# A graph layer with its edges in sorted order: one quad of hot nodes moved to the end of the list

## The chip, the core and the metric

The kernel runs on one core of one Trainium2 chip. The metric is the device time of one execution in microseconds (us). The engines have short names: PE is TensorE (matmul), PEld its weight loads, DVE is VectorE, ACT is ScalarE, POOL is GpSimd and SP is SyncE, which issues most transfers. Each engine takes its own instructions in order and waits for others through semaphores.

## The reference

There are 12,500 nodes of 128 features and 400,000 edges, sorted by destination. A destination is 12500 times the square of a uniform number, so nodes with low numbers are hot: they have many edges. Each edge has a length. Only edges shorter than 10 have any effect, which are 71,145 of these inputs.

```python
rbf = jnp.exp(-(distances[:, None] - centers) ** 2 / (2.0 * width * width))
cut = 0.5 * (jnp.cos(jnp.pi * distances / CUTOFF) + 1.0) * (distances <= CUTOFF)
W = (jax.nn.silu(rbf @ fw1 + fb1) @ fw2 + fb2) * cut[:, None]
messages = (h[src] @ pw + pb) * W
agg = jax.ops.segment_sum(messages, dst, num_segments=num_atoms)
y = h + (jax.nn.silu(agg @ mw1 + mb1) @ mw2 + mb2)
out = _layernorm(x + y)          # h is x
```

## The kernel before

**Packing.** Seven chunks of edges (bounds QB = 0, 13, 24, 46, 69, 91, 114, 141 in quads) are compacted on DVE: the edges shorter than 10 are put in order, and written are their source rows (`srci`), places among nodes (`dl`, `f_dl`), lengths (`near_d`), cut factors (`cut`) and the base node of each half quad (`base_i`). Chunks 1 to 6 are packed beside the main loop.

**The main loop** has NL = 139 steps, one for each quad of 4 x 128 edges. POOL gathers the rows of proj = x@pw + pb, one indirect DMA for 128 edges (L1048), four to a quad; for eight quads, named in `SINGLY`, one of the four is fetched row by row through SP instead (L1038). ACT makes the radial functions for two quads at a time (L1094, L1095), PE multiplies by fw1 (L1103), ACT applies silu (L1109), PE multiplies by fw2 with the bias (L1117, L1120), and DVE multiplies by the gathered rows, which gives the message (L1131; for the last quad in four pieces). DVE also builds a one-hot matrix of destinations times the cut factor (`hot`, L1143, in `place`). PE multiplies message by one-hot into PSUM (`sums`, L1163, in `sum_up`), and DVE adds the result to aggT, which holds all nodes' sums, at a base read into a register (L1196, in `add`). The two halves of a quad have a base each. `added(q)` says up to which quad the additions have come at step q, and `keep_busy` puts filler matmuls into PE's queue (L1350).

**Node blocks.** Since the edges are sorted, a tile of 128 nodes is final once the quads that reach it are added. From step 70 on, blocks of nodes run beside the edges: `node_first` (PE L1204 and L1205, then silu on ACT L1209), `node_second` (PE L331, L334), `node_stats` (DVE L1225, which forms 2x + y, and the statistics L1230), `deviations` (L1237 to L1241, the last on ACT), `scales` (L1248, L1249, whose result is `by`), and `normalize` (DVE or POOL L1260, or ACT L1263, and the store L173). Blocks are four tiles; the last ones, in `TAIL`, have 4, 4, 2, 3, 2 and 3 tiles and start at tiles 80, 84, 88, 90, 93 and 95; they are called by these numbers. Tile 97, the last one, has 84 nodes. `READY` gives how many steps ahead of the end a block's first product is put into the queue.

**The end.** After the loop stand the last quad's addition, blocks 90, 93 and 95, and a branch (`tc.If(some > 0)`, L1640) round a general path, which these inputs don't take. Ahead of it stands a hint on the branch for each of five engines.

The order on each engine is that in which the Python code calls these functions; a clock kept by the planner places the packing work and the gathers between them.

Of the kernel before, what the change touches and what calls it, by code (L numbers as in the profile page):

```python
# [20 lines left out]
P = 128  # L21
# [22 lines left out]
NL = 139  # L44
AHEAD = 3
# [25 lines left out]
SINGLY = (22, 45, 62, 67, 86, 102, 118, 133)  # L71
# [7 lines left out]
READY = {80: 9, 84: 6, 88: 5, 90: 3, 93: 2}  # L79
# [4 lines left out]
def kernel(  # L84
# [57 lines left out]
    x_sb, loaded = {}, [0]  # L142

# [6 lines left out]
    def rows(t0, n=None):  # L150
        n = n or TAIL.get(t0, 4)
        return [min(P, N - t * P) for t in range(t0, min(t0 + n, NT))]
# [15 lines left out]
    def node_dma(t0, sb, dr, store, n=None, eng=nc.sync):  # L168

        for a, m, k in alike(rows(t0, n)):  # L170
            d = dr[(t0 + a) * P:(t0 + a) * P + m * k].rearrange("(p t) f -> p t f", p=k)
            s = sb[:k, a:a + m]
            eng.dma_start(d, s) if store else eng.dma_start(s, d)  # L173

# [636 lines left out]
    def unpack(c):  # L811
# [69 lines left out]
        def later(more=0.0):  # L881

            if c or known[0] >= DIRECT // QT:
                awake[c] = clock[0] + (5.0 if known[0] >= QB[c + 1] else 1.0 if c == 0 else 2.5) + more
# [31 lines left out]
        known[0] = QB[c + 1]  # L916
        yield 0
        mine = [q for q in SINGLY if QB[c] <= q < QB[c + 1]]
        if mine:
            at_row = work.tile([64, P], I32, name="at_row", bufs=2)  # L920
            nc.vector.tensor_scalar(at_row[:np_], f_src[:, :P], float(4 * H), None, op0=OP.mult)
            for q in mine:
                p = 2 * (q - QB[c])
# [16 lines left out]
        nc.vector.tensor_scalar(f_dl, part, base, None, op0=OP.subtract)  # L940
        yield from to_places(f_dl, dl)
# [22 lines left out]
        nc.vector.scalar_tensor_tensor(inside, f_dl, float(WIDTHS[c]), inside, op0=OP.is_lt, op1=OP.mult,  # L964
# [77 lines left out]
    def fetch(q, idx=None, table=None, js=range(QT)):  # L1042
        got = quad_sb[place_of(q) if q >= 0 else 0]
        for j in js:
            if q in SINGLY and j == 0:
                continue
            i = srci[:, 2 * q + j // 2, j % 2:j % 2 + 1] if idx is None else idx[:, j:j + 1]
# [24 lines left out]
    def radials(to):  # L1072

        while next_o[0] < min(to, -(-NL // 2)):
# [3 lines left out]
            a, b = 4 * o, 2 * quads(o)[-1] + 2  # L1078
# [3 lines left out]
    def chunk_of(q):  # L1082
        return max(c for c in range(NC_) if QB[c] <= q)
# [54 lines left out]
    def place(q):  # L1138

        hot = own(q, "hot", 1)  # L1140
        for j in reversed(range(QT)):
            at = 2 * q + j // 2, slice(j % 2, j % 2 + 1)
# [26 lines left out]
    def base_of(q, ks=(0, 1)):  # L1169
        for k in ks:  # L1170
            if k == windows(q):
                break
            _, v = nc.values_load_multi_w_load_instructions(  # L1173
                base_i[0:1, 2 * q + k:2 * q + k + 1], engines=[mybir.EngineType.DVE],
# [4 lines left out]
    def bases_of(q0, q1):  # L1179

        _, v = nc.values_load_multi_w_load_instructions(
            base_i[0:1, 2 * q0:2 * q1], engines=[mybir.EngineType.DVE],
# [91 lines left out]
    def finish(every):  # L1274

        for t0 in every:
# [6 lines left out]
            normalize(*ready.pop(0))  # L1283
# [3 lines left out]
    blocks = [*range(0, min(TAIL), 4), *TAIL]  # L1287
# [8 lines left out]
    def nodes(q):  # L1296
# [5 lines left out]
        for k, t0 in enumerate(early):  # L1302
            if begin[t0][0] - 5 == q:
                load_x(t0)
            if begin[t0][2] == q:
                if k % 4 == 0:
                    st_of[0] = statistics()
                node_stats(t0, st_of[0][:, k % 4 * 4:])
# [14 lines left out]
        if q == NL - 3:  # L1323
            node_stats(88, st_of[3][:, 8:])
            dev_of.append(deviations([84, 88], st_of[3][:, 4:]))
            nc.scalar.activation(warm, half_pi, AF.Silu)
        if q == NL - 2:
            node_second(90)
            for k in (1, 2):
                st_of[k] = statistics()  # L1330
            scales(*dev_of.pop(0))
            for _ in (84, 88):
                normalize(*ready.pop(0))

    st_of, deep, dev_of = {}, [], []

    def tail(q):

        for t0, k in READY.items():
            if q == NL - k:  # L1340
                assert done_to(2 * added(q + 1)) >= (t0 + TAIL[t0]) * P
# [49 lines left out]
    def pack_until(us, among=2):  # L1391

        while clock[0] < us and todo and todo[0] < among:
            have = [c for c in todo[:3] if c < among and (c == 0 or c - 1 in sent or c == todo[0])]
            have.sort(key=lambda c: 0 if c in sent and known[0] < QB[c + 1] else 1)
# [69 lines left out]
    while known[0] < QB[2]:  # L1465
# [21 lines left out]
    for q in range(NL - 1):  # L1487
# [3 lines left out]
        if q == NL - 2:  # L1491
            bases_of(q, NL)
# [21 lines left out]
        if q > NL - 5:  # L1514
            keep_busy(2)
        sum_up(q, msg)
        now = range(added(q), added(q + 1))
        for k in now if q < NL - 2 else ():
            base_of(k, (0,))
        if q < NL - 2:  # L1520
            place(q + 1)
        if q == NL - 4:
            place(NL - 1)
        if q == NL - 2:
            for j in range(QT):
                sum_up(NL - 1, message(NL - 1, (j, j + 1)), (j,))
        for k in now:
            if q < NL - 2:
                base_of(k, (1,))
# [11 lines left out]
        if todo:  # L1541
            pack_until(max(there_at[q + 1], clock[0] + (PACK_US if known[0] >= QB[3] else EARLY_US)), NC_)
# [7 lines left out]
    add(NL - 1)  # L1550
    node_first(95)
    node_stats(90, st_of[1])
    node_second(93)
    tc.mark_branch_hint_location("rest", some, [
# [123 lines left out]
```

## Time and profile before

| | us |
|---|---|
| median of 3 runs | 723.49 |
| lowest and highest | 722.11 and 725.21 |
| the profiled execution | 723.36 |
| its span in the trace | 721.6 |
| busy time of POOL in the span | 534.3 (74%) |
| busy time of PE, DVE, ACT | 588.0, 560.8, 399.6 |

The mean granted clock of PE was 0.912. A row of the timeline has the start, the time it took, the engine, the line, the operation, output and inputs, the shape, how many such instructions the row stands for, and in brackets how long the engine had been idle before it and what ended that. A row of the windows has the stretch, its length, the busy time (and number) of PE, PE's weight loads, DVE, ACT and POOL, the granted clock of PE (1.00 is full rate), the busy share of the DMA engines and GB/s.

### The profile page before, as it was taken

The numbers are of one execution on the slowest core, as the hardware profiler recorded it, in microseconds if no ns is written. First come the engines' busy times: TensorE is split into PE (matmuls) and PEld (weight loads), VectorE is DVE, ScalarE is ACT, GpSimd is POOL, SyncE is SP. The second block draws the span as 40 slices with busy tenths as digits, with TensorE's granted clock in tenths as the row PEclk, the third lists the DMA queues.
The fourth block names the chain that finished last, engine by engine and source line by source line (L and its number), as shares of the span: only waits on it lengthen the run. The fifth ranks groups of instructions, "written<-read, shape, count | busy, mean of one in ns | idle before, by whom it ended". The sixth has DMA issues, their size and how long they took to land.

```text
span 721.6 us, 13649 instructions
## 1 busy us (share of the span) xinstructions
PE 588.0 (81%) x3519; PEld 462.7 (64%) x3519; DVE 560.8 (78%) x1737; ACT 399.6 (55%) x569; POOL 534.3 (74%) x572
## 2 busy tenths in 40 slices
PE   6777787898888878788498898999977878888974
PEld 6766455776766657667376676777755656556753
DVE  8898879787988999899589996868555545655684
ACT  6547624474545576465338355859744744574483
POOL 7777777777777777777777777777777777777771
PEclk9999786998988999999769998999997989999997
DMA  8996433334333433342333343544433433255242
GB/s 273 331 303 196 143 115 86 79 110 125 97 101 87 127 98 105 99 126 86 98 102 112 101 117 101 148 124 141 128 97 112 142 99 99 82 170 138 63 141 66
DMA packets 53103, 91.37 MB, mean 127 GB/s; under 512 B 13824, under 2 KB 20576, under 8 KB 53018
## 3 DMA queue, kind: packets, MB, share of 16 engines
q1 hardware_dynamic: 34466, 53.20, 22.1%
q0 software_dynamic: 17840, 36.77, 20.2%
q8 instruction: 29, 0.48, 0.3%
q10 hardware_dynamic: 712, 0.46, 0.2%
q14 instruction: 56, 0.46, 0.2%
HBM read 74.59 MB, written 15.79 MB: 125 GB/s over the span
## 4 chain that ended last, share of the span: by engine, by line
DVE 30%; PE 24%; DMA 14%; issue 13%; POOL 11%; ACT 4%; DVEq 2%; SPq 0%; ACTq 0%; POOLq 0%
POOL quad L1048 11%; DMA quad<-proj,srci 9%; PE ph L1103 7%; DVE hot L1143 5%; PE bank L1120 5%; PE sums L1163 5%; DVE msg L1131 3%; PE bank L334 3%; DVE aggT L1196 2%; DVE r_d L509 2%; DVE bank L515 2%; DVEq L1173 2%; PE bank L1117 2%; DVE nodes L519 2%; DVE quad L1143 1%
## 5 line engine op out<-in xcount | busy, mean ns | idle before, releaser
L1048 POOL DMA_INDIRECT quad<-proj,srci x421 | 400.0, 950 | 128.4 <-issue 105.5
L1120 PEld LDWEIGHTS bank<-fw_sb,s 128*128 128x128 f32 x1112 | 159.3, 207 | 69.3 <-issue 62.1
L1109 ACT ACTIVATE s<-ph 128x1024 f32<-128x1024 f32 x70 | 71.3, 1018 | 176.5 <-PE ph L1103 176.4
L1120 PE MATMUL bank<-fw_sb,s 128*128 128x128 f32 x1112 | 159.7, 290 | 0.0
L1103 PE MATMUL ph<-rbf,w_sb 102*128 102x512 f32 x278 | 146.7, 653 | 7.7 <-ACT rbf L1095 3.8
L1163 PEld LDWEIGHTS sums<-hot,msg 128*128 128x128 f32 x816 | 109.5, 200 | 57.7 <-issue 27.6
L1143 DVE TENSOR_SCALAR hot<-iota_n,dl,cut 128x80 f32<-128x80 f32 (+4 forms) x408 | 108.3, 339 | 24.7 <-PE sums L1163 22.2
L1163 PE MATMUL sums<-hot,msg 128*128 128x80 f32 (+4 forms) x816 | 111.3, 281 | 17.7 <-DVE msg L1129 10.0
L1117 PE MATMUL bank<-fb_b,ones_b 96*128 96x512 bf16 x139 | 56.0, 403 | 50.9 <-DVE msg L1131 31.0
L1048 POOL DMA_INDIRECT x<-proj,srci x79 | 74.8, 947 | 24.1 <-issue 20.1
L1131 DVE TENSOR_TENSOR msg<-bank,quad 128x512 f32<-128x512 f32 (+1 forms) x82 | 55.5, 676 | 40.3 <-DMA quad<-proj,srci 36.0
L1103 PEld LDWEIGHTS ph<-rbf,w_sb 102*128 102x128 f32 x278 | 52.5, 210 | 48.1 <-issue 38.7
L1196 DVE TENSOR_TENSOR aggT<-aggT,sums 128x80 f32 (+4 forms) x209 | 53.7, 257 | 30.9 <-PE bank L1205 11.7
L1094 ACT ACTIVATE rbf<-d,rbf_bias,rbf_scale 102x512 f32<-102x512 f32 x70 | 56.2, 803 | 20.1 <-DMA d<-near_d 20.1
L1048 POOL DMA_INDIRECT quad<-in_x_dram,srci x48 | 48.1, 1003 | 15.5 <-issue 12.5
L334 PEld LDWEIGHTS bank<-pw_sb,xT 128*128 128x128 f32 (+1 forms) x292 | 42.1, 208 | 8.0 <-issue 4.2
L1095 ACT ACT_TABLE_LOAD x35 | 44.9, 1283 | 0.6
L1109 ACT ACT_TABLE_LOAD x35 | 44.9, 1283 | 0.6
L1131 DVE TENSOR_TENSOR quad<-bank,quad 128x512 f32<-128x512 f32 (+2 forms) x40 | 25.3, 632 | 25.6 <-DMA quad<-proj,srci 21.6
L1095 ACT ACTIVATE rbf<-rbf 102x512 f32<-102x512 f32 x70 | 44.1, 630 | 1.5
L334 PE MATMUL bank<-pw_sb,xT 128*128 128x128 f32 (+1 forms) x292 | 42.6, 293 | 0.6 <-ACT xT L984 0.6
L1143 DVE TENSOR_SCALAR quad<-iota_n,dl,cut 128x128 f32<-128x128 f32 (+3 forms) x148 | 40.6, 352 | 3.0 <-issue 1.8
(273 smaller groups left out, 803.8 us busy)
## 6 DMA issues: line engine op xcount, KB each, us to landing
d<-near_d SPq DMA_DIRECT2D x70, 256.0 KB
dl<-proj SPq DMA_DIRECT2D x1024, 0.5 KB
x<-in_x_dram SPq DMA_DIRECT2D x46, 256.0 KB
quad<-proj,srci POOLq DMA_INDIRECT x421
proj<-hp SPq DMA_DIRECT2D x24, 256.0 KB
out_dram<-x SPq DMA_DIRECT2D x22, 256.0 KB
r_d<-in_edge_weight_dram SPq DMA_DIRECT2D x5, 256.0 KB
r_dst<-in_dst_dram SPq DMA_DIRECT2D x5, 256.0 KB
```

What stands on the lines that cost most here:

```text
L334: nc.tensor.matmul(to[:m, k, :], lT[:, k * P:k * P + m], w, start=False, stop=(k == a + c - 1))
L1048: ins = nc.gpsimd.indirect_dma_start(out=got[:, j, :], out_offset=None, in_=proj if table is None else table, in_offset=bass.IndirectOffse ...
L1094: nc.scalar.activation(rbf[:u], d[:u], AF.Square, bias=rbf_bias[:u], scale=rbf_scale[:u])
L1095: nc.scalar.activation(rbf[:u], rbf[:u], AF.Exp, scale=-1.0 / (2.0 * width * width))
L1103: nc.tensor.matmul(ph[:, h, :], w1_sb[:2 * KR, h, :], rbf[:2 * KR], start=True, stop=True)
L1109: nc.scalar.activation(s[:, :n], ph[:, :n], AF.Silu)
L1117: nc.tensor.matmul(pu, ones_b[:, :P], bias_b["fb2"].rearrange("k j f -> k (j f)"), start=True, stop=False)
L1120: nc.tensor.matmul(pu[:, j * H:(j + 1) * H], s[:, j * P:(j + 1) * P], fw2_sb, start=False, stop=(j == QT - 1))
L1131: nc.vector.tensor_mul(msg[:, a:b, :], pu_of[q].rearrange("p (j f) -> p j f", j=QT)[:, a:b, :], got_of[q][:, a:b, :])
L1143: nc.vector.tensor_scalar(hot[:, j, :wide(q)], iota_n[:, :wide(q)], dl[:, at[0], at[1]], cut[:, at[0], at[1]], op0=OP.is_equal, op1=OP.mult)
L1163: ins = nc.tensor.matmul(pa[:, k * W:k * W + wide(q)], msg[:, j, :], hot[:, j, :wide(q)], start=(j % n == 0), stop=(j % n == n - 1))
L1196: nc.vector.tensor_add(to, to, pa[:, k * W:k * W + wide(q)])
```

## The change

Quad 26, whose edges go to nodes 437 to 472, all in tile 3, leaves its place and becomes the last step, 138 (`LAST`, `quad_of`, `steps`); every quad behind it is handled one step earlier. Tile 3 is therefore not part of block 0 any more but a block of its own (`END`, one tile), loaded near the end and done last. Chunk 2's check of places gets narrower bounds for quad 26, in four small DVE operations (`that`, `lim`, `upto`). Since block 95 no longer waits for the last quad, blocks 90, 93 and 95 go ahead, between the messages of the last two quads: block 90's statistics ahead of step 137's one-hot (`late_nodes`), 93 and 95 between the four pieces of the last message (`last_step`). Blocks 93, 95 and END have one common group of deviations. Block 88 and block 90 are normalised on POOL, and so is 93. The fillers of the steps NL-3 and NL-2 are gone. The last quad's sums have one window, 80 nodes wide, where they had two of 128. The hint on the branch is given for DVE, PE and POOL only, and the general path ends in one `finish(blocks)` where it had three.

```diff
-SINGLY = (22, 45, 62, 67, 86, 102, 118, 133)
+SINGLY = (22, 44, 62, 67, 86, 102, 118, 133)
-READY = {80: 9, 84: 6, 88: 5, 90: 3, 93: 2}
+READY = {80: 9, 84: 6, 88: 5, 90: 4, 93: 3}
+LAST = 26
+END = 3
+SIZES = {0: 3, END: 1, **TAIL}
...
+    def quad_of(q):
+        return q if q < LAST or q >= NL else LAST if q == NL - 1 else q + 1
...
+    def late_nodes():
+        node_stats(90, st_of[3][:, 10:])
+        deep.append(deviations([84, 88, 90], st_of[3][:, 4:]))
+        nc.scalar.activation(warm, half_pi, AF.Silu)
+        st_of[1] = statistics()
+    def last_step(q, msg):
+        bases_of(q, NL - 1)
+        tc.mark_branch_hint_location("rest", some, [
+            mybir.EngineType.DVE, mybir.EngineType.PE, mybir.EngineType.Pool])
+        sum_up(q, msg)
+        scales(*deep.pop(0))
+        node_second(93)
+        def last(j):
+            sum_up(NL - 1, message(NL - 1, (j, j + 1)), (j,))
+        normalize(*ready.pop(0))
+        last(0)
+        add(q)
+        last(1)
+        node_first(95)
+        node_stats(93, st_of[1])
+        last(2)
+        node_second(95)
+        for n in (2, 3):
+            normalize(*ready.pop(0), on=range(n), v=nc.gpsimd)
+        last(3)
+        add(NL - 1)
+        node_first(END)
+        node_stats(95, st_of[1][:, 2:])
+        node_second(END)
+        node_stats(END, st_of[1][:, 5:])
+        scales(*deviations([93, 95, END], st_of[1]))
+        normalize(*ready.pop(0), on=(0, 1), v=nc.gpsimd)
+        normalize(*ready.pop(0), on=(0, 1), eng=nc.scalar)
+        normalize(*ready.pop(0), on=(0,))
...
-        if q > NL - 5:
+        if q == NL - 4:
             keep_busy(2)
+        if q == NL - 3:
+            node_second(90)
         sum_up(q, msg)
...
+        if q == NL - 3:
+            late_nodes()
+        place(q + 1)
...
-    add(NL - 1)
-    node_first(95)
-    node_stats(90, st_of[1])
-    node_second(93)
-    tc.mark_branch_hint_location("rest", some, [
-        mybir.EngineType.SP, mybir.EngineType.Activation, mybir.EngineType.DVE,
-        mybir.EngineType.PE, mybir.EngineType.Pool])
-    node_stats(93, st_of[1][:, 3:])
-    node_second(95)
-    early_dev = deviations([90, 93], st_of[1])
-    node_stats(95, st_of[2], lambda: scales(*early_dev))
-    normalize(*ready.pop(0), on=(0, 1, 2), v=nc.gpsimd)
-    normalize(*ready.pop(0))
-    last_dev = deviations([95], st_of[2])
-    scales(*last_dev)
-    normalize(*ready.pop(0), on=(0, 1), eng=nc.scalar)
+    last_step(NL - 2, message(NL - 2))
```

PE's queue round the sums of step 137, before (those of `hot_1188`; `quad_79` and `quad_77` are the last quad's, `bank` with `zs` is a node block's second product, `bank` with `aggT` its first):

```order
L334 MATMUL bank_167<-mw_sb,zs 128x128 x3
L1350 LDWEIGHTS ones_b
L1350 MATMUL ph<-mb_b,ones_b 128x512
L1350 LDWEIGHTS ones_b
L1350 MATMUL ph<-mb_b,ones_b 128x512
L1163 MATMUL sums<-hot_1188,msg_1216 128x128 x4
L1163 MATMUL sums<-quad_79,quad_77 128x128 x4
L1204 LDWEIGHTS mb_b
L1204 MATMUL bank_165<-ones_b,mb_b 128x256
L1205 MATMUL bank_165<-aggT,mw_sb 128x256
```

and now (the sums of step 137 are those of `hot_1189`, and `hot_1070` is step 136's; L343 and L346 are the second product, L1228 and L1229 the first, L1187 the sums):

```order
L346 MATMUL bank_166<-mw_sb,zs 128x128 x3
L1187 MATMUL sums<-hot_1070,msg_1075 128x128 x4
L1228 LDWEIGHTS mb_b
L1228 MATMUL bank_168<-ones_b,mb_b 128x256
L1229 MATMUL bank_168<-aggT,mw_sb 128x256
L1187 MATMUL sums<-hot_1189,msg_1217 128x128 x4
L343 LDWEIGHTS ones_b
L343 MATMUL bank_166<-mb_b,ones_b 128x256
L346 MATMUL bank_166<-mw_sb,zs 128x128 x2
L1187 MATMUL sums<-quad_80,quad_78 128x80 x2
```

Block 90's second product (x3) has moved ahead of the sums of step 136, the fillers are gone, block 93's first product stands ahead of the sums of step 137 and its second one ahead of the last quad's, whose first two pieces follow.

DVE's queue from the message of step 136 (`msg_1074`) to the one-hot of step 137, before:

```order
L1131 TENSOR_TENSOR msg_1074<-bank_165,quad_82 128x512
L1225 SCALAR_TENSOR_TENSOR x_93<-x_93,bank_167 128x256
L1230 BN_STATS st<-x_93 128x6 x2
L1237 TENSOR_TENSOR dif<-st 128x6
L1238 TENSOR_TENSOR both_m<-st 128x12
L1239 SCALAR_TENSOR_TENSOR dif<-dif 128x6
L1240 TENSOR_TENSOR v<-both_m,dif 128x6
L1173 TENSOR_LOAD base_i
L1143 TENSOR_SCALAR hot_1188<-iota_n,dl,cut 128x128 x4
```

and now (x_94 is block 88, x_87 block 90):

```order
L1155 TENSOR_TENSOR msg_1075<-bank_166,quad_83 128x512
L1249 SCALAR_TENSOR_TENSOR x_94<-x_94,bank_168 128x256
L1254 BN_STATS st<-x_94 128x6 x2
L1197 TENSOR_LOAD base_i
L1249 SCALAR_TENSOR_TENSOR x_87<-x_87,bank_166 128x384
L1254 BN_STATS st<-x_87 128x6 x3
L1261 TENSOR_TENSOR dif<-st 128x9
L1262 TENSOR_TENSOR both_m<-st 128x18
L1263 SCALAR_TENSOR_TENSOR dif<-dif 128x9
L1264 TENSOR_TENSOR v<-both_m,dif 128x9
L1295 MEMSET st 128x96
L1167 TENSOR_SCALAR hot_1189<-iota_n,dl,cut 128x128 x4
```

Block 90's addition and statistics, three tiles, have come in between, and a memset.

SP's queue ahead of the branch, before (x_86 is block 90, normalised on POOL, and x_87 block 93, on ACT):

```order
L173 DMA out_dram<-x_91 128x512
L173 DMA out_dram<-x_92 128x512
L173 DMA out_dram<-x_93 128x256
L173 DMA out_dram<-x_86 128x384
L173 DMA out_dram<-x_87 128x256
L1640 COMPARE_AND_BRANCH
```

and now (x_88 is block 93, normalised on POOL, and `end` the single tile, on DVE):

```order
L177 DMA out_dram<-x_92 128x512
L177 DMA out_dram<-x_93 128x512
L177 DMA out_dram<-x_94 128x256
L177 DMA out_dram<-x_87 128x384
L177 DMA out_dram<-x_88 128x256
L177 DMA out_dram<-end 128x128
L1680 COMPARE_AND_BRANCH
```

The last two stores are now those of blocks whose factors come from the last, common group.

90 lines of the change are left out of this document (44 added, 46 removed).

## The prediction

> **What bounds the kernel now.** I read the page first, for the engine that is never free for long; then busy time by windows, for the body and for the end; then the timeline of the last 24 us; then the instructions recorded at the final branch.
>
> ```profile
> L1048 POOL DMA_INDIRECT quad<-proj,srci x421 | 400.0, 950 | 128.4 <-issue 105.5
> ```
>
> and of the windows of 100 us (busy time of PE, PE's weight load, DVE, ACT and POOL; granted clock; DMA share; GB/s):
>
> ```profile
> 600.00:700.00 100.00, 83.51 (x482) 62.85 (x480) 63.56 (x218) 55.38 (x86) 75.62 (x81) 0.93 0.40 118
> ```
>
> POOL issues the gathers, four to a quad, one every 0.95 us with 0.30 us ahead of each (128.4 / 421) that waits for nothing. The last full window shows this pace as a fixed share: 75.62 us of 100 on POOL, which is 0.95 / 1.25. Nothing that PE, DVE or ACT do in the body shortens the run as long as POOL is not made to wait. What follows POOL's last gather is another matter:
>
> ```profile
> 697.98 0.69 DVE L1131 TENSOR_TENSOR msg<-bank,quad 128x512 f32<-128x512 f32 x1 [0.69 <-DMA quad<-proj,srci]
> 698.73 1.16 PE L1163 MATMUL sums<-hot,msg 128*128 128x128 f32 x8 [0.51 <-DVE msg L1131]
> 700.65 1.11 DVE L1143 TENSOR_SCALAR hot<-iota_n,dl,cut 128x128 f32<-128x128 f32 x4 [0.52 <-issue]
> 702.53 0.69 DVE L1131 TENSOR_TENSOR msg<-bank,quad 128x512 f32<-128x512 f32 x1 [0.24 <-DMA quad<-proj,srci]
> 703.83 1.16 PE L334 MATMUL bank<-mw_sb,zs 128*128 128x128 f32 x6 [0.41 <-ACT zs L1209]
> 704.78 1.06 PE L1350 MATMUL ph<-mb_b,ones_b 96*128 96x512 bf16 x2
> 704.88 0.94 POOL L1048 DMA_INDIRECT quad<-proj,srci  x1 [0.30 <-issue]
> 705.64 1.91 PE L1163 MATMUL sums<-hot,msg 128*128 128x128 f32 x8
> 707.47 0.29 DVE L1131 TENSOR_TENSOR quad<-bank,quad 128x128 f32<-128x128 f32 x1 [1.06 <-DMA quad<-proj,srci]
> 709.21 0.61 DVE L1196 TENSOR_TENSOR aggT<-aggT,sums 128x128 f32 x2 [0.94 <-PE bank L1205]
> 709.74 0.55 DVE L1225 SCALAR_TENSOR_TENSOR x<-x,bank 128x384 f32<-128x384 f32 x1
> 709.88 0.84 PE L1205 MATMUL bank<-aggT,mw_sb 128*128 128x340 f32 x2 [0.56 <-DVE aggT L1196]
> 710.32 0.68 DVE L1230 BATCH_NORM_STATS2 st<-x 128x6 f32<-128x128 f32 x3
> 710.81 0.52 ACT L1209 ACTIVATE zs<-bank 128x256 f32<-128x256 f32 x2 [1.16 <-PE bank L1205]
> 711.25 0.71 PE L334 MATMUL bank<-mw_sb,zs 128*128 128x128 f32 x4
> 711.31 0.42 DVE L1225 SCALAR_TENSOR_TENSOR x<-x,bank 128x256 f32<-128x256 f32 x1 [0.31 <-PE bank L334]
> 711.76 0.49 DVE L1230 BATCH_NORM_STATS2 st<-x 128x6 f32<-128x128 f32 x2
> 712.80 0.61 DVE L1225 SCALAR_TENSOR_TENSOR x<-x,bank 128x256 f32<-128x256 f32 x2
> 713.63 0.67 DVE L1230 BATCH_NORM_STATS2 st<-x 128x6 f32<-128x128 f32 x3
> 713.90 1.32 POOL L1260 TENSOR_SCALAR x<-x,rs,by 128x128 f32<-128x128 f32 x3 [8.08 <-ACT dev L1241]
> 714.33 0.20 DVE L1237 TENSOR_TENSOR dif<-st 128x3 f32<-128x3 f32 x1
> 715.13 0.30 ACT L1241 ACTIVATE dev<-v,eps 128x3 f32<-128x3 f32 x1 [0.50 <-DVE v L1240]
> 715.67 0.16 DVE L1249 SCALAR_TENSOR_TENSOR by<-both_m,rs 128x3 f32<-128x3 f32 x1
> 716.50 1.06 ACTq L173 DMA_DIRECT2D out_dram<-x  x2
> ```
>
> POOL's last gather ends at 705.82 and the span at 721.6, so the edit plays for these 15.8 us. Three stretches lie in them. From 704.8 to 709.8 PE and DVE finish the sums of the last two quads. Then the last three blocks pass through PE, ACT and DVE, and the last scale factors (by) stand at 715.67 + 0.16 = 715.83. Then come stores, and a stretch in which no engine computes:
>
> ```profile
> L1640 SPq EVENT_SEMAPHORE  x9: 17/17/17, 719.3 to 719.9; - x9
> L1640 POOLq EVENT_SEMAPHORE  x5: 17/43/43, 714.4 to 714.8; - x5
> ...
> L1640 ACTq EVENT_SEMAPHORE  x2: 17/17/17, 720.2 to 720.3; - x2
> ...
> L1640 POOLq COMPARE_BRANCH  x1: 70/70/70, 713.9 to 713.9; - x1
> ...
> L1640 SPq COMPARE_BRANCH  x1: 70/70/70, 716.1 to 716.1; - x1
> L1640 ACTq COMPARE_BRANCH  x1: 68/68/68, 717.6 to 717.6; - x1
> ```
>
> At the branch round the fallback SP is silent from 716.1 to 719.3 and ACT from 717.6 to 720.2; POOL takes only 0.5 us. SP's remaining work ends the span 2.3 us after it resumes (721.6 - 719.3). So whatever makes SP reach its branch earlier counts in full, and ACT's lateness (720.2) is 1.4 us from the end.
>
> **The body, part by part.** Taking quad 26 out of its place removes four gathers there and adds four at the end: 4 x 1.25 us each way, sum zero. The four added DVE operations of one element per row, in chunk 2's unpacking, are far smaller than any row above and lie on an engine that is not the bound: nothing. What is no longer covered is that chunks 3 to 6 are wanted one quad, 5.0 us, earlier. The closest of those I looked at is chunk 3:
>
> ```profile
> 223.32 0.24 DVE L907 CAST srci<-bank 128x92 int32<-128x92 f32 x1
> ...
> 242.94 0.94 POOL L1048 DMA_INDIRECT quad<-proj,srci  x1 [0.30 <-issue]
> ```
>
> Its row numbers are ready at 223.56 and quad 46's first gather starts at 242.94: 19.4 us of cover, of which 14.4 remain. Nothing for the body, up to +3 us if the packing on DVE slips further than that.
>
> **The tail, step by step.** (1) DVE up to the message of step 137. That message now follows block 90's addition and statistics, 0.55 + 0.68 = 1.23 us, on an in-order queue. Before, it ended at 702.53 + 0.69 = 703.22; the 0.24 us for which it waited for its gather absorbs one memset and the small gaps. It ends at 704.4, 1.2 us late. (2) PE. The two fillers of 1.06 us at 704.78 are gone, and block 90's second product is ahead of the previous sums. The eight sums can start at 704.5 instead of 705.64, and at the duration of their row (1.91) end at 706.4; the two adds of 0.61 end at 707.1. Before they ended about 708.3, so the step gains 1.2 us. (3) DVE now does three message pieces (0.29 each) and block 93's addition and statistics (0.42 + 0.49) before the last add: 707.1 + 1.78 plus gaps = 709.1. On PE the last piece's sum stands behind block 95's first product (0.84), its silu on ACT (0.52) and second product (0.71): 708.0 + 0.84 + 0.52 + 0.71 = 710.1. The last add is one instruction, half of 0.61, and ends at 710.5. Before: 709.82. The step gives back 0.7 us plus what (2) gained. (4) After it DVE does block 95 (0.61 + 0.67), the single tile (half of 0.42 and of 0.49: 0.5), the deviations (714.33 to 715.13: 0.8) and the factors (715.13 to 715.83: 0.7). 710.5 + 3.3 = 713.8, where before there was 715.83: 2.0 us earlier. That is the change's gain; the single tile's own products and silu hide under block 95's addition and statistics. (5) The way to SP's branch is longer. Before it was 0.3 us past the factors. Now POOL normalises two tiles of block 93 only after the common factors: 0.2 us to start, 2 x 1.32 / 3 = 0.88, then two stores queue on SP:
>
> ```profile
> L173 SPq DMA_DIRECT2D out_dram<-x x25: 332/370/377, 452.6 to 715.7; - x25
> ```
>
> 2 x 0.37 and the gaps: 713.8 + 0.2 + 0.88 + 0.87 = 715.75 against 716.1. Gain left: 0.4 us. ACT's branch follows its 84-row tile and the two stores (0.5 + 1.06): 715.4 instead of 717.6, which SP hides. (6) SP's silence of 3.1 us and its 2.3 us stay. Sum: a span of 721.6 - 0.4 = 721.2. The profiled run took 723.36, 1.76 above its span and 0.13 below the median of 723.49, so the forecast is 723.1.
>
> **The clock.** The sums at 698.73 took 1.16 us and those at 705.64 took 1.91. The windows show why:
>
> ```profile
> 697.57:700.98 3.41, 1.97 (x13) 1.13 (x12) 2.37 (x10) 1.29 (x3) 2.65 (x3) 1.00 0.81 245
> 700.98:704.40 3.42, 1.65 (x8) 0.96 (x9) 2.62 (x12) 2.97 (x6) 2.66 (x3) 1.00 0.25 62
> 704.40:707.81 3.41, 3.41 (x17) 2.98 (x16) 0.93 (x4) 2.20 (x6) 1.12 (x2) 0.50 0.39 130
> 707.81:711.22 3.41, 2.85 (x19) 1.99 (x18) 2.15 (x8) 0.79 (x3) 0.00 (x0) 1.00 0.09 29
> ```
>
> After a window with PE busy for 1.65 of 3.42 us the granted clock is 0.50 for one window; after 1.97 of 3.41 it stays 1.00. In the changed kernel PE waits for DVE from about 701.0 (sums of step 136 done) to 703.8 (first product of block 93), so I keep one half-clock window in the same place, and that is why step (2) used 1.91. At 1.16 there, and with block 93's second product quicker likewise, the tail would be about 1.2 us shorter. [...]
>
> **Rivals.** *No half-clock window*: its phase against the program is luck, and a gap of 2.8 us need not fill half of a window. 723.1 - 1.2 = 721.9; chance 0.13. *SP's silence goes*: at its branch SP jumped over 287 instructions, counted in the compiled program, and was silent 3.1 us; POOL jumped over 77 and lost 0.5. The changed program makes it 169 for SP and 197 for ACT, between the two. If 169 is short enough, ACT's branch ends it: 715.45 + 2.6 + 1.2 = 719.3, that is 721.2; if neither is silent, SP's 715.75 + 2.3 = 718.1, that is 720.0, and without the slow window 718.8. [...] Chance 0.20. [...] That SP's and ACT's hints are dropped should cost nothing, since with them both were silent.
>
> *Half clock to the end* (the other side): without fillers and with PE waiting on DVE, the window after 707.8 is granted 0.50 too. On the chain then lie block 95's two products (0.84 + 0.71), a piece's sum and the single tile's products, some 2.3 us, which at the ratio 1.91 / 1.16 = 1.65 cost 1.5 more: 724.6. If the window before 704.4 is slow as well, the second product of block 90 and the sums of step 136 (1.16 each) delay DVE's whole queue: by 0.65 x 2.3 = 1.5 us again, and with the waits in between 727.3. It decides where PE is under half busy in two windows running. For it: 1.65 of 3.42 was already under. Against: from 707.8 PE has three blocks to do. Chance 0.15, about 0.06 of it above 727.1. *POOL waits* for chunk 3 or another (728 or more): 0.07. *The change doesn't do what it says*, above all that the check on quad 26's nodes sends the program into the fallback, hundreds of us: nodes 437 to 472 all lie in tile 3, and the rest is small: 0.05 with everything unnamed.
>
> **How the numbers follow.** The forecast's own case has 0.40. A measurement of this kernel can tell about 0.5%, 3.6 us: 719.9 and 727.1 are the borders. Faster: half of the case without SP's silence (0.11), some of the quick-clock case and the unnamed (0.04): 0.15. Slower: 0.06 of half clock, 0.07 of POOL, 0.03 unnamed: 0.16. Same: 0.69. The range leaves out the two extremes, about a tenth on each side: 719.0 to 727.3.
>
> **What would show it.** Right: POOL's last gather still ends within 0.5 us of 705.8; the message of step 137 starts about 703.7; no L1350 filler near 704; the last factors at 713.5 to 714.1; SP's branch 1.9 us behind them and about 3 us of silence after it. Wrong: POOL gaps above 1 us before 700; SP resuming within 0.6 us of its branch; a granted clock of 0.50 in two adjoining windows between 701 and 712; or the message of step 137 as early as 702.5, which would mean that block 90 is not ahead of it.

## The result, and the profile after

The changed kernel takes 722.94 us (median of 17 runs, 720.72 to 728.44), the kernel before 723.49 (17 runs, 721.34 to 725.6). The ratio is 0.9994, with a 95% interval of 0.998 to 1.0008: no difference. The profiled execution took 725.23 us, its span is 723.5 us. Five of the experiments below (before_again, after_again, no_branch, fill, and later swap_norm) ran on occasions when every execution took about 1000 us, that of the kernel before too, with POOL standing still in the body (idle ahead of its gathers for 290.4 us in after_again, for 128.4 in before). Of them only the last 25 us are read; all gathers had ended ahead of that. swap_norm, early_hint, late_90, before_nofill and short_branch were executed once each, and one execution does not tell a microsecond apart: they are read by their profiles alone.

The timeline of the changed kernel's tail:

```profile
698.08 0.61 DVE L1220 TENSOR_TENSOR aggT<-aggT,sums 128x128 f32 x2
699.67 0.69 DVE L1155 TENSOR_TENSOR msg<-bank,quad 128x512 f32<-128x512 f32 x1 [0.98 <-DMA quad<-proj,srci]
...
700.24 0.38 PE L1141 MATMUL bank<-fb_b,ones_b 96*128 96x512 bf16 x1 [0.58 <-ACT zs L1233]
...
702.38 0.55 DVE L1249 SCALAR_TENSOR_TENSOR x<-x,bank 128x384 f32<-128x384 f32 x1 [1.17 <-PE bank L346]
...
705.74 0.69 DVE L1155 TENSOR_TENSOR msg<-bank,quad 128x512 f32<-128x512 f32 x1
...
706.42 0.95 POOL L1071 DMA_INDIRECT quad<-proj,srci  x1 [0.30 <-issue]
...
706.87 1.92 PE L1187 MATMUL sums<-hot,msg 128*128 128x128 f32 x8
...
712.61 0.24 DVE L1220 TENSOR_TENSOR aggT<-aggT,sums 128x80 f32 x1 [1.58 <-PE sums L1187]
...
716.16 0.17 DVE L1273 SCALAR_TENSOR_TENSOR by<-both_m,rs 128x6 f32<-128x6 f32 x1
...
716.49 1.06 POOL L1284 TENSOR_SCALAR x<-x,rs,by 128x128 f32<-128x128 f32 x2 [6.90 <-ACT dev L1265]
...
717.57 0.33 SPq L177 DMA_DIRECT2D out_dram<-x  x1
718.00 0.40 SPq L177 DMA_DIRECT2D out_dram<-end  x1
```

and what it records at the branch:

```profile
L1680 SPq EVENT_SEMAPHORE  x9: 17/17/17, 721.1 to 721.7; - x9
...
L1680 ACTq EVENT_SEMAPHORE  x2: 17/17/17, 720.9 to 721.0; - x2
...
L1680 ACTq COMPARE_BRANCH  x1: 50/50/50, 718.1 to 718.1; - x1
L1680 SPq COMPARE_BRANCH  x1: 50/50/50, 718.4 to 718.4; - x1
```

POOL's last gather ends at 707.37 us, 1.5 later than before. That is not the change's doing in the loop: POOL had one long wait near the start, where before it waited 0.95 us:

```profile
70.84 0.94 POOL L1071 DMA_INDIRECT quad<-in_x_dram,srci  x1 [3.45 <-PE bank L346]
```

In later executions of kernels with the same body the last gather ended at 704.2 to 705.5 us (with the body of before at 704.1 and 704.4), and the long wait was not there. To compare tails I count from the addition of step 135, the last point that both kernels share. In the timeline of before it is

```profile
696.69 0.60 DVE L1196 TENSOR_TENSOR aggT<-aggT,sums 128x128 f32 x2
```

| us after the addition of step 135 begins | before | changed |
|---|---|---|
| message of step 137 begins | 5.84 | 7.66 |
| end of POOL's last gather | 9.13 | 9.29 |
| last addition ends | 13.13 | 14.77 |
| last factors stand | 19.14 | 18.25 |
| SP's branch | 19.4 | 20.3 |
| end of the span | 24.9 | 25.4 |

The factors come 0.9 us earlier, and the way from them to the end takes 7.2 us instead of 5.8. In these two profiles the gain is made and given back.

### The profile page after: what moved, and what is told of

It is laid out like the page before. It is cut to its first block, busy times and chain, and to the rows that moved or that the text cites. A ratio compares the mean times of both kernels' runs of the same rounds, so it can differ in the third digit from the quotient of the medians.

```text
span 723.5 us, 13653 instructions
## 1 busy us (share of the span) xinstructions
PE 590.4 (82%) x3519; PEld 467.5 (65%) x3519; DVE 559.8 (77%) x1736; ACT 397.7 (55%) x564; POOL 535.5 (74%) x576
## 4 chain that ended last, share of the span: by engine, by line
PE 29%; DVE 20%; DMA 17%; issue 12%; POOL 11%; ACT 5%; SPq 3%; DVEq 2%; ACTq 0%; POOLq 0%
DMA quad<-proj,srci 9%; POOL quad L1071 9%; PE ph L1127 8%; PE bank L1144 6%; PE sums L1187 5%; DVE hot L1167 4%; PE bank L346 3%; DVE msg L1155 2%; DVE aggT L1220 2%; PE bank L1229 2%; PE bank L1141 2%; DMA proj<-hp 2%; SPq L1061 2%; DVE bank L527 2%; DMA x<-in_x_dram 1%
## 5 line engine op out<-in xcount | busy, mean ns | idle before, releaser
L1144 PEld LDWEIGHTS bank<-fw_sb,s 128*128 128x128 f32 x1112 | 162.8, 210 | 68.9 <-issue 62.1
L1144 PE MATMUL bank<-fw_sb,s 128*128 128x128 f32 x1112 | 163.0, 294 | 0.0
L1127 PE MATMUL ph<-rbf,w_sb 102*128 102x512 f32 x278 | 143.8, 642 | 7.6 <-ACT rbf L1119 3.8
L1187 PEld LDWEIGHTS sums<-hot,msg 128*128 128x128 f32 x816 | 112.6, 205 | 54.6 <-issue 25.5
L1187 PE MATMUL sums<-hot,msg 128*128 128x80 f32 (+4 forms) x816 | 114.0, 286 | 16.5 <-DVE msg L1153 9.6
L346 PEld LDWEIGHTS bank<-pw_sb,xT 128*128 128x128 f32 (+1 forms) x292 | 43.6, 214 | 6.8 <-issue 3.4
L346 PE MATMUL bank<-pw_sb,xT 128*128 128x128 f32 (+1 forms) x292 | 43.6, 298 | 0.5 <-ACT xT L1007 0.5
L1167 DVE TENSOR_SCALAR quad<-iota_n,dl,cut 128x104 f32<-128x104 f32 (+3 forms) x148 | 40.4, 348 | 3.8 <-issue 2.8
```

What stands on the lines that cost most here:

```text
L346: nc.tensor.matmul(to[:m, k, :], lT[:, k * P:k * P + m], w, start=False, stop=(k == a + c - 1))
L1127: nc.tensor.matmul(ph[:, h, :], w1_sb[:2 * KR, h, :], rbf[:2 * KR], start=True, stop=True)
L1144: nc.tensor.matmul(pu[:, j * H:(j + 1) * H], s[:, j * P:(j + 1) * P], fw2_sb, start=False, stop=(j == QT - 1))
L1167: nc.vector.tensor_scalar(hot[:, j, :wide(q)], iota_n[:, :wide(q)], dl[:, at[0], at[1]], cut[:, at[0], at[1]], op0=OP.is_equal, op1=OP.mult)
L1187: ins = nc.tensor.matmul(pa[:, k * W:k * W + wide(q)], msg[:, j, :], hot[:, j, :wide(q)], start=(j % n == 0), stop=(j % n == n - 1))
```

## The experiments

**The tail again: before_again and after_again.** Both kernels unchanged.

> The kernel before, unchanged, profiled once more. 'Tail' here and below is the span's end minus the end of POOL's last gather: 721.6 - 705.82 = 15.8 us in the first profile of before and 723.5 - 707.37 = 16.1 us in that of the changed kernel. Theory A (the spread between executions, 721.3 to 725.6 us, arises ahead of the gathers or in single gaps between them, and the tail is steady): the last gather ends more than 0.5 us off 705.82 and the tail is 15.4 to 16.2. Rival B (the tail varies with the phase of the clock's window): the tail is off 15.8 by more than 0.7 us while the last gather stays where it was.

> The changed kernel, unchanged, profiled once more and timed. Theory A: the gap of 3.45 us at 70.8 us was an accident of that execution, the last gather ends within 1 us of 705.8, and the tail is again 15.8 to 16.4 us, so that the change did not shorten the tail, and the 0.5 us between the medians is not the 0.4 us of the prediction. Rival B: the tail is 15.4 or less, as predicted, and the first profile was the accident. Timed: ratio to before 0.998 to 1.001 under both.

Measured: from the message of step 136 to the end it takes 24.70 us (before) and 23.45 us (changed); in the first profiles it was 23.60 and 23.78. So neither theory holds as it was put: the tails are not steady, they vary by 1.1 and 0.3 us, and the granted clock goes with it. In before_again 0.50 is granted over two windows running inside the tail (975.9 to 982.7 us), and the factors stand 20.1 us after the addition of step 135; in after_again, from 0.2 us after that addition on, in none ahead of the factors, and they stand 17.11 us after it (991.95 - 974.84), not 18.25:

```profile
974.84 0.61 DVE L1220 TENSOR_TENSOR aggT<-aggT,sums 128x128 f32 x2 [1.03 <-PE sums L1187]
...
991.78 0.17 DVE L1273 SCALAR_TENSOR_TENSOR by<-both_m,rs 128x6 f32<-128x6 f32 x1
```

So the factors' gain is not one number: 0.9 us in the first pair of profiles, 3.0 in this one. Measured from the last gather's end nothing can be said, since in these two executions all gathers had landed early. The timed ratio of after_again on that occasion was 1.011 (1.0047 to 1.0177), against 0.9994 in the main comparison. Why the body went otherwise there was not settled.

**The silence behind the branch.** Four kernels. First, no branch at all, and no hint on it:

```diff
-    with tc.If(some > 0, label="rest"):
-        ...
```

> The changed kernel without the branch and the general path behind it (left out: what runs when the lists don't hold all edges). Theory: SP's silence of 2.7 us behind its branch is the fetch of the instructions it jumps to; without the jump the tail falls from 16.1 to 13.2-13.6 us and the ratio to before is about 0.996. Rival: the silence is a wait for the last stores to land, which stands at the end of the program anyway; then the tail stays above 15.3 us and the ratio at 0.999.

The last factors and the span in no_branch:

```profile
core 0 of [0], span 1003.8 us
...
999.15 0.17 DVE L1273 SCALAR_TENSOR_TENSOR by<-both_m,rs 128x6 f32<-128x6 f32 x1
```

From the factors (999.32) to the end it takes 4.5 us, where after_again has 7.3: 2.9 us less, as the theory says. The stores were landing in the silence, and not the cause of it. The timed ratio, 1.0115 (1.0021 to 1.0209), equals that of the changed kernel on the same occasion, where 0.996 was expected against before; with intervals of 1% to each side it says nothing on 3 us.

Then the branch with next to nothing behind it:

```diff
     with tc.If(some > 0, label="rest"):
-        total = ...
-        ...
-        finish(blocks)
+        finish([END])
```

> The changed kernel with the general path cut down to one block's products (left out: all else that runs when the lists don't hold all edges), so that SP jumps over about 4 instructions and ACT over 5 instead of 169 and 197. Theory (the distance decides): no silence, SP and ACT resume within 0.6 us of the branch, and from the last factors to the end it takes 4.5 to 5.0 us. Rival (a taken branch costs SP and ACT this time at any distance): silence 2.5 to 3.2 us.

```profile
L1680 SPq EVENT_SEMAPHORE  x2: 17/17/17, 718.4 to 718.5; - x2
...
L1680 ACTq COMPARE_BRANCH  x1: 45/45/45, 717.9 to 717.9; - x1
L1680 ACTq EVENT_SEMAPHORE  x1: 17/17/17, 718.1 to 718.1; - x1
L1680 SPq COMPARE_BRANCH  x1: 50/50/50, 718.2 to 718.2; - x1
```

SP and ACT go on 0.2 us after the branch, and the end comes 4.6 us behind the factors. So the distance decides: a jump over 4 instructions costs SP 0.2 us, one over 169 costs 2.7. The trace also shows what goes on in the silence. Among the transfers of the changed kernel between 718.2 and 721.1 us are two on the queue that the profile calls instruction, both between 719.3 and 720.0:

```profile
q14 instruction: 2, 0.02, 1.8%
```

after_again, swap_norm and late_90 have two such transfers in their silences as well; short_branch has none from 714 us on. By the queue's name instructions are fetched there. The two transfers are over by 720.0, 1.1 us before SP goes on, so the fetch as the trace has it does not fill the 2.7 us, and what the rest is stays open. Then the branch as it was, with a hint far ahead:

```diff
+        if q == 120:
+            early_some = nc.values_load(bad_i[0:1, 2:3], ..., engines=[SP, Activation])
+            tc.mark_branch_hint_location("rest", early_some, [SP, Activation])
```

> The changed kernel with one more register load and one hint on the branch for SP and ACT at step 120, some 100 us ahead of the branch (the kernel before had them 20 us ahead, the changed one has none). Theory (the silence behind the branch is the fetch of the instructions jumped to, and a hint helps only if the engine fetches a block of instructions between hint and branch): SP's and ACT's silence falls from 2.7-2.9 us to under 0.7 us, and from the last factors to the end of the span it takes 4.6 to 5.0 us instead of 7.3. Rival: a hint on SP and ACT does nothing wherever it stands; silence 2.5 to 3.2 us.

```profile
L1686 SPq EVENT_SEMAPHORE  x9: 17/17/17, 715.3 to 716.4; - x9
...
L1686 ACTq EVENT_SEMAPHORE  x2: 17/17/17, 714.8 to 714.9; - x2
...
L1686 ACTq COMPARE_BRANCH  x1: 68/68/68, 714.4 to 714.4; - x1
L1686 SPq COMPARE_BRANCH  x1: 73/73/73, 714.7 to 714.7; - x1
```

The silence is 0.55 us on SP and 0.48 on ACT, as the theory says, and no transfer of instructions falls into it. By what means the hint does this is not shown. The way from the factors (712.57) to the end (718.1) is 5.5 us, 1.8 shorter than in after_again and not the 2.3 to 2.7 expected. The first row shows where the rest went: SP's nine waits now spread over 1.1 us, where they took 0.6. SP waits for the last stores to land (the last one lands 3.72 us past the factors, SP's last wait comes 3.8 us past them), which the silence had covered. The one execution took 719.86 us, beside 723.0 of before; the hint is not worth that much, for the last gather ended at 704.22 here and at 705.52 in short_branch, which took 722.45. The same hint in the kernel before:

> The kernel before with the hint on the branch for SP and ACT moved from 20 us ahead of the branch to step 120, about 100 us ahead, and nothing of the change. Theory (the hint's place alone takes the silence away, 3.16 us on SP in the profile of before): SP and ACT resume within 0.7 us; the end then follows ACT's branch, which is 1.5 us behind SP's, and the last factors are followed by 4.2 to 4.6 us instead of 5.8; ratio to before 0.9975 to 0.9985. [...]

```profile
L1645 SPq EVENT_SEMAPHORE  x9: 17/17/17, 714.8 to 717.3; - x9
...
L1645 SPq COMPARE_BRANCH  x1: 73/73/73, 714.3 to 714.3; - x1
L1645 ACTq COMPARE_BRANCH  x1: 68/68/68, 715.8 to 715.8; - x1
```

The silence is gone here too (0.55 us), but the waits spread over 2.5 us, and ACT's stores are issued later than SP's: ACT's branch, behind its stores, stands at 715.8, SP's at 714.3. From the factors (714.00) to the span's end (719.1) it takes 5.1 us, 0.7 less than before, where 1.2 to 1.6 were expected. The ratio is 0.9995 (0.998 to 1.0009): not to be told from none.

**The way to SP's branch: swap_norm.**

```diff
-        normalize(*ready.pop(0), on=(0, 1), v=nc.gpsimd)
-        normalize(*ready.pop(0), on=(0, 1), eng=nc.scalar)
+        normalize(*ready.pop(0), on=(0, 1))
+        normalize(*ready.pop(0), on=(0, 1), v=nc.gpsimd, eng=nc.scalar)
```

> The changed kernel with two of the last normalisations exchanged: block 93's two tiles on DVE, whose store SP issues, and block 95's two full tiles on POOL, whose stores ACT issues. Theory (SP's branch sets the end, and it is reached 2.1 us past the last factors because POOL's two tiles and SP's two stores stand in a row): SP's branch comes 1.4 to 1.6 us past the factors and the tail (end of POOL's last gather to the end of the span, 16.1 us in the profile of the changed kernel) falls by 0.5 to 0.7 us. Rival: ACT, whose stores now wait for POOL, reaches its branch 2.4 us past the factors instead of 1.8 and takes over the end; then the tail falls by less than 0.3 us.

```profile
997.60 0.17 DVE L1273 SCALAR_TENSOR_TENSOR by<-both_m,rs 128x6 f32<-128x6 f32 x1
...
L1680 SPq COMPARE_BRANCH  x1: 50/50/50, 999.3 to 999.3; - x1
L1680 ACTq COMPARE_BRANCH  x1: 50/50/50, 1000.3 to 1000.3; - x1
```

SP's branch stands 1.6 us past the factors instead of 2.1 (18.29 - 16.12 in after_again, both from the message of step 136), and from that message the end comes at 22.90 us instead of 23.45: 0.55 us less, as the theory says. POOL's two tiles and SP's two stores do cost the way to the branch 0.5 us. At the end it is less sure, since the silence varies too: from the factors to the end it takes 6.8 us here, and 7.0 to 7.3 in the four profiles without the exchange (after, after_again, fill, late_90).

**The steps ahead of the sums.** late_90 puts block 90's statistics back behind the message of step 137:

```diff
-        if q == NL - 3:
-            late_nodes()
         place(q + 1)
...
         sum_up(q, msg)
-        scales(*deep.pop(0))
+        late_nodes()
         node_second(93)
         def last(j): ...
-        normalize(*ready.pop(0))
         last(0)
         add(q)
+        scales(*deep.pop(0))
+        normalize(*ready.pop(0))
         last(1)
```

> The changed kernel with block 90's addition, statistics and deviations behind the message of step 137 instead of ahead of the one-hot of step 137. Step (1) of the prediction holds if the message of step 137 then starts 4.0 to 5.2 us after the addition of step 135 begins, instead of 7.66 (both profiles of the changed kernel), and PE's sums of step 137 come as much earlier. Theory: the last factors then come about 1 us earlier, since DVE had been waiting for PE's sums behind that message and does block 90 in that wait. Rival: DVE's work is only moved, the last factors come within 0.3 us of 17.1 us after the addition of step 135 at full clock (996 us execution: 16.12 + 0.99).

```profile
696.84 0.61 DVE L1220 TENSOR_TENSOR aggT<-aggT,sums 128x128 f32 x2
...
702.57 0.69 DVE L1155 TENSOR_TENSOR msg<-bank,quad 128x512 f32<-128x512 f32 x1
...
703.31 1.16 PE L1187 MATMUL sums<-hot,msg 128*128 128x128 f32 x8
...
706.92 1.63 ACT L1287 ACTIVATE x<-x,by,rs 128x128 f32<-128x128 f32 x4
...
708.46 0.48 ACT L1233 ACTIVATE zs<-bank 128x256 f32<-128x256 f32 x2
...
710.10 0.24 DVE L1220 TENSOR_TENSOR aggT<-aggT,sums 128x80 f32 x1 [2.47 <-PE sums L1187]
...
713.95 0.17 DVE L1273 SCALAR_TENSOR_TENSOR by<-both_m,rs 128x6 f32<-128x6 f32 x1
```

The message of step 137 starts 5.73 us after the addition of step 135, not 7.66 (the 4.0 to 5.2 expected was too bold), and the factors stand at 17.28 us, against 17.11 at full clock with the work in its place. So the rival holds: moving the work back gains nothing. (Of the 17.28 us 0.3 come from a window at 0.50 that fell on the single tile's second product, 0.79 us instead of 0.49; without it the factors would stand about 0.1 us ahead of 17.11.) The rows show what is late instead: block 84's factors come in one group with block 90's, so ACT's normalisation of block 84 (706.92, 1.63 us) now stands ahead of block 95's silu (708.46), and PE's last piece stands behind block 95's second product. In this arrangement the message of step 137 is not what holds up the end; an arrangement that moves block 90 without making ACT late was not run.

before_nofill takes the fillers from the kernel before:

```diff
-        if q > NL - 5:
+        if q == NL - 4:
             keep_busy(2)
```

> The kernel before without the fillers of the steps NL-3 and NL-2 (four matmuls of 512 columns), one part of the change alone. Theory (step 2 of the prediction: the fillers stood on the path): the sums of step 137 begin right behind block 90's second product or behind the message, about 0.9 us earlier than before counted from the message of step 136 (7.66 us), and the last factors come 0.5 to 1.0 us earlier than 17.84 us after that message. Rival: the granted clock falls to 0.50 in one more window, and the factors come later than before.

```profile
696.45 0.69 DVE L1131 TENSOR_TENSOR msg<-bank,quad 128x512 f32<-128x512 f32 x1 [0.65 <-DMA quad<-proj,srci]
...
704.33 1.22 PE L1163 MATMUL sums<-hot,msg 128*128 128x128 f32 x8
...
714.07 0.16 DVE L1249 SCALAR_TENSOR_TENSOR by<-both_m,rs 128x3 f32<-128x3 f32 x1
```

Neither answer came. The sums of step 137 begin 7.88 us after the message, not earlier than 7.66, because the window at 0.50 fell 1.6 us earlier, counted from that message, and made block 90's second product slow instead (1.65 us for 1.16). The factors stand at 17.78 us, against 17.84. What the fillers cost is hidden by the clock and by the last gathers, for which the message pieces wait; the gain that I put down to their going is not shown.

**The clock: fill.** Eight fillers in PE's idle stretch behind the sums of step 136:

```diff
             add(k)
+        if q == NL - 3:
+            keep_busy(8)
         tail(q)
```

> The changed kernel with eight filler matmuls on PE behind the sums of step 136, ahead of block 93's first product, where PE sat idle from 703.3 to 705.9 us. Theory (the half-clock window from 705.9 to 709.3 follows from that idle stretch): the granted clock stays 1.00, the sums of step 137 take 1.05 us instead of 1.92, block 93's second product 0.6 instead of 0.9, the last add comes 1.2 us earlier and the tail is 14.9 us; ratio 0.997. Rival 1 (the window has another cause): sums still at 1.9 and tail 16.1. Rival 2 (the fillers run into the product's way): block 93's first product starts over 0.3 us later than 0.65 us after the add of step 136 began, and the gain is below 0.6 us.

Not decided: the clock stayed at 1.00 up to the factors, which came 17.10 us after the addition of step 135, but after_again without fillers had the same on that occasion. Shown is only that the fillers are in nobody's way (rival 2 falls): the message of step 137 came at 7.65 us as without them. The timed ratio, 1.0028 (0.9978 to 1.0077), is below the changed kernel's 1.0112 of that occasion, but the two intervals overlap. The windows of the changed kernel and, below them, of early_hint (busy time of PE first, granted clock third from the end):

```profile
702.55:705.96 3.41, 0.88 (x9) 0.60 (x7) 3.27 (x16) 1.59 (x3) 2.75 (x3) 1.00 0.43 135
705.96:709.37 3.41, 3.41 (x14) 3.13 (x15) 1.53 (x7) 3.29 (x7) 3.05 (x7) 0.50 0.15 38
```

```profile
699.25:702.66 3.41, 1.47 (x14) 1.19 (x12) 2.80 (x14) 0.94 (x1) 2.56 (x3) 1.00 0.44 140
702.66:706.07 3.41, 2.79 (x18) 2.18 (x19) 2.60 (x11) 3.37 (x8) 2.95 (x6) 1.00 0.15 38
```

PE waits about 2.5 us in both. In the first the wait lies inside one window, 0.88 us busy, and the next has 0.50; in the second it is split over two and none has. The window's phase against the program differs from execution to execution: counted from the beginning of the addition of step 135, a window begins after 7.88 us in the first profile (705.96 - 698.08), after 7.19 in early_hint (702.66 - 695.47) and after 9.35 in no_branch (990.19 - 980.84). Of the seven profiles in which PE's queue is the changed kernel's (its own, after_again, no_branch, short_branch, early_hint, swap_norm, hint_swap), the first, no_branch and short_branch had a window at 0.50 between the addition of step 135 and the factors. It costs 1.1 to 1.4 us up to the factors (18.2 to 18.5 against 17.11). That the phase alone decides is not shown. short_branch is like the first, but in no_branch the wait was split as well, 0.7 and 1.9 us, and the window with the longer part was followed by 0.50 although PE was busier in it than in early_hint's:

```profile
986.78:990.19 3.41, 1.55 (x10) 1.25 (x11) 2.89 (x13) 3.05 (x5) 0.42 (x1) 1.00 0.00 0
990.19:993.60 3.41, 3.41 (x14) 2.79 (x14) 2.08 (x8) 1.83 (x6) 1.74 (x5) 0.50 0.21 77
```

And in late_90, whose order is another, 0.50 followed a window with PE busy for 2.13 us:

```profile
707.71:711.12 3.41, 2.13 (x16) 1.47 (x15) 1.02 (x5) 1.37 (x6) 0.86 (x2) 1.00 0.37 131
711.12:714.53 3.41, 0.79 (x2) 0.50 (x2) 2.18 (x12) 2.10 (x4) 0.25 (x1) 0.50 0.15 52
```

**Put together: hint_swap and hint_swap_fill.** The edits of early_hint and swap_norm, and in the second also that of fill.

> The changed kernel with the early hint and with the exchange of the two normalisations (block 93's on DVE, block 95's on POOL). Theory (both shorten the same path, from the last factors to SP's last wait): from the factors to the end 4.9 to 5.1 us, where the early hint alone had 5.5 and the changed kernel 7.1 to 7.3; ratio to before 0.995 to 0.9975. Rival: ACT's branch, 2.5 us past the factors, ends it, and the exchange brings less than 0.2 us.

> The same with eight filler matmuls where PE waits for DVE behind the sums of step 136. Theory (an idle stretch of 2.5 us that fills most of a window of the clock is followed by a window at 0.50, which cost 1.1 us up to the last factors: 18.24 against 17.11 us from the addition of step 135): no window at 0.50 between the addition of step 135 and the last factors, which come 17.1 us apart, and a median 0.3 to 0.8 us below that of the kernel without fillers. Rival: the fillers change nothing that shows, since the window falls behind the sums in only some of the executions.

The branch in hint_swap:

```profile
L1686 SPq EVENT_SEMAPHORE  x9: 17/17/17, 714.1 to 716.3; - x9
...
L1686 SPq COMPARE_BRANCH  x1: 73/73/73, 713.6 to 713.6; - x1
L1686 ACTq COMPARE_BRANCH  x1: 68/68/68, 714.4 to 714.4; - x1
```

hint_swap: 722.53 us, ratio 0.9976 (0.996 to 0.9992). From the factors (712.05) to the end 5.95 us, not less than the 5.5 of early_hint: the exchange brings nothing, as the rival has it, but it is not ACT's branch that ends it. With the silence gone SP's nine waits spread over 2.2 us, and the last one that takes time ends when ACT's last store lands: by the trace's semaphores it lands at 716.21, and SP goes on at 716.23. The exchange brings SP's branch forward, but not the last store, which is issued 1.72 us past the factors with it and 1.67 without. So what was worth 0.5 us under the silence is worth nothing without it. Whether it costs 0.4 is not shown: the last store lands 4.16 us past the factors here and 3.72 in early_hint, but 4.2 in the first profile of the changed kernel and in after_again, which don't have the exchange. hint_swap_fill: 721.16 us, ratio 0.9959 (0.9944 to 0.9973), the only one below both kernels beyond the intervals (that of the changed kernel is 0.998 to 1.0008), if only by 0.4% of before's time. Its factors stand 17.1 us after the addition of step 135, with no window at 0.50 between. That its median is 1.4 us below hint_swap's fits the theory of the fillers, but the two intervals overlap and both profiles show full clock, so it is not settled. Not run: early hint and fillers without the exchange; whether that is better still is not known.

## Why the prediction was right, and where it was not

The forecast was 723.1 us and no change; measured were 722.94 and no change. The frame held: the body goes at POOL's pace (busy for 75.72 us of 100 from 600 to 700 us, before for 75.62), chunk 3 came in time, and all is decided behind the last gather. Within it several terms were off and cancelled.

- **Step 1**, the message of step 137 1.2 us later: measured from the last gather's end 1.7 us (3.29 us ahead of it before, 1.63 now). Missing was a wait for a PSUM bank: the product for the last quad waited 0.58 us for ACT's silu of block 90 (700.24), and block 90's second product stands behind it, for which DVE waited 1.17 us (702.38). late_90 showed that undoing the step gains nothing at the end, since ACT is late then.
- **Step 2**, 1.2 us gained because the fillers are gone: the sums began 0.50 us ahead of the last gather's end (before 0.18), not 1.3, and before_nofill shows no gain from the fillers' going. Of the 0.8 us missing, 0.5 is the late message; the rest is block 93's first product, which stands ahead of the sums and took 1.20 us at the clock of 0.50, where in after_again, at full clock, it took 0.70.
- **Step 3**, last addition 4.7 us behind the last gather's end: measured 5.5 (before 4.0). The step itself was sized well, 6.0 us from the start of the sums to the end of the last addition predicted and measured; it began 0.8 us late.
- **Step 4**, factors 2.0 us earlier: 1.0 us counted from the last gather, 0.9 from the addition of step 135. The work behind the last addition was right (3.3 predicted, 3.48 measured); the loss is that of steps 1 and 2.
- **Step 5**, 1.95 us from the factors to SP's branch: 2.1 measured. POOL's two tiles took 1.06 us and not 0.88, while DVE was normalising beside it (716.36 to 717.22). swap_norm confirmed this path to the branch by shortening it.
- **Step 6**, 3.1 us of silence: 2.7 on SP. That saved the 0.4 us which the tail would otherwise have been longer.

From the last gather to the end the tail was to fall from 15.8 to 15.4 us and measured 16.1 in the profile with a window at 0.50. The medians differ by 0.55 us in the other direction, inside the interval, so the agreement of 723.1 with 722.94 is closer than the working deserved, and in part luck. The forecast reckoned with a window at 0.50 in the tail. Three of seven profiles have it, and there the factors stand 18.2 to 18.5 us after the addition of step 135. In the four others they stand at 17.1, which is 2.0 earlier than the 19.14 of before's first profile: the gain that was forecast, but without the window that it was forecast with. That the medians nevertheless hardly differ fits what the way to the end costs, 7.1 to 7.3 us past the factors in three profiles of the changed kernel's end (after, after_again, fill) against 5.6 to 6.1 in before, before_again and before_nofill.

**The rivals.** *SP's silence goes* did not come by the shorter jump: over 169 instructions SP was still silent for 2.7 us. The chance of 0.20 was an estimate; at what distance the silence goes was not shown when it was made. That distance matters is shown by short_branch (4 instructions, 0.2 us), that a hint 100 us ahead takes the silence away by early_hint and before_hint (0.55 us on SP in both), and that instructions are fetched in it by the two transfers there. What I had wrong is the reason for which dropping the hints should cost nothing: with hints 20 us ahead SP was silent for 3.16 us in before, but with one 100 us ahead for 0.55. *No half-clock window* had 0.13 and came in four of seven profiles; its price, 1.2 us, was nearly right (1.1 to 1.4). *Half clock to the end* did not come. *POOL waits* came in one execution, with the 3.45 us at 70.8 us and the last gather 1.5 us late in the first profile; in the later ones it did not.

## What to carry to other kernels

When a chain at the end is shortened, follow it to the last instruction of the engine that ends the program: here the 0.9 us gained at the last factors in the first pair of profiles was lost because the last stores now queue behind POOL, on the one queue that ends the run (SP's branch 2.1 us past the factors, before 0.3; SP's last wait at 721.7, ACT's at 721.0). A silence in which no engine computes (2.7 us here) is a term like any other; look what happens in it, because it also covers things (the landing of the stores), and an edit that pays under the cover can be worth nothing without it (the exchange of the two normalisations: 0.55 us less with the silence, 5.95 us against 5.5 from the factors to the end without). With windows of the clock of 3.4 us and a tail of 16, one profile is one draw: read the tail in several.

## What the runs showed of the hardware

- A jump over 169 instructions silenced SP for 2.7 us and one over 4 for 0.2. A branch hint about 100 us ahead of it brought the 2.7 to 0.55 us. With hints only 20 us ahead, the kernel before was silent for 3.16 us at a jump over 287; the same kernel without any hint was not run. In four profiles with the long silence (after, after_again, swap_norm, late_90) two transfers on the instruction queue fall into it, in early_hint and short_branch none. By what means the early hint works was not shown.
- The granted clock fell to 0.50 after a window with PE busy for 0.88 us of 3.41, and in the kernel before after 1.65 of 3.42, but stayed 1.00 after 1.47 of 3.41. In late_90 it fell even after 2.13 of 3.41. So busy time as the trace has it does not decide alone, and the prediction's limit of about half a window does not hold; what decides was left open.
- Without silence, SP's last waits follow the stores' landing: in hint_swap ACT issued the last store just ahead of its branch at 714.4, it landed at 716.21, and SP's waits ended at 716.3.
